# Selective-scan kernel: a Sign whose loops are exchanged, and a copy of partial sums issued one place earlier on ScalarE

## The chip, the cores and the metric

One core of one Trainium2 chip. The metric is device time in microseconds (us); the executions of one kernel on one chip spread over 0.05% to 0.43%, mostly over 0.3% or less. Each kernel was run beside the kernel before on the same chip, in alternating rounds; the kernel before has medians of 5773.73 to 5782.82 us by chip, so comparisons are made within rounds. Engines in profiles: PE is TensorE's matmuls, PEld its weight loads, DVE VectorE, ACT ScalarE, POOL GpSimd, SP SyncE.

## The reference, cut to what matters

The network has a binarised convolution block with a selective scan, then linear attention and a small feed-forward part, on 4 images of 64 x 64 pixels and 96 channels. The change touches two places:

```python
t = prelu(conv3x3(sign(xc)) + b) + xc          # 192 channels, 4096 pixels an image
xconv = silu(t)                                # u of the scan
x_dbl = sign(xconv) @ Wb.T + b                 # only the SIGN of xconv feeds the projections

h = exp(delta * A) * h + (delta * u) * B       # the scan along the 4096 pixels, 4 directions, 192 x 16 states
y = sum over the 16 states of h * C
```

## The kernel before

A work item ("piece") of the scan is one tile of 128 x 1024: 32 channels by 4 states on the partitions, 1024 pixels. There are 1536 pieces. Per piece i:

```python
if i >= 1: self.carry(i - 1)            # ACT copies the last column of h(i-1): waits for scan i-1
if i + 1 < n: self.decay(i + 1)         # ACT: dA = exp(delta * A), into one of two PSUM tiles
full = i % 8 == 3 and i > 8
if full: self.evacuate(i - 4)           # ACT copies 8 pieces' sums of y out of their PSUM bank
elif i >= 3: self.reduce(i - 3)         # PE sums over the states into that bank
if i + AHEAD < n: self.inject(i + AHEAD)  # POOL: w = (delta * u) * B
self.scan(i)                            # DVE: the scan; then w = h * C on DVE or on POOL
...
interleave(lanes); next(back, None)     # background: one step of other stages' work
if full: self.reduce(i - 3)             # in a full iteration the sums come last
```

Who computes `w = h * C` is decided while the program is built: a tally of modelled times gives it to the less loaded of VectorE and GpSimd (905 and 631 of the 1536). The "background" holds the convolutions of the next images and the epilogues of earlier ones, in steps between pieces. The first image's convolution has nothing to hide under: no scan can start before it ends.

The convolution works through 16 parts an image (96 channels x 512 pixels, 18 matmuls each). For each part, while the next part's matmuls are issued:

```python
vector: pz = pz * s + v;  pz = r * (1 - a) + pz
scalar: sg = Sign(pz)     -> fp8 bytes, even and odd pixels of 64 put apart    # the changed line
scalar: e = Exp(-pz); e = Ln(e + 1); e = Exp(-e)                               # sigmoid
vector: u = pz * e
...                       # then, for the part whose matmuls have ended:
vector or scalar: v = ...;  scalar: r = Relu(...)       # read the matmuls' result
```

## Time and profile before

| | before |
|---|---|
| time | 5783.25 us (5775.27 to 5783.98, 3 runs) |
| first convolution, start of first to end of last part | about 83 to 217 us |
| scans | 288 to 5610 us |
| VectorE and GpSimd busy in the scans | 94% each |
| ScalarE busy in the scans | 65% |
| the Sign | 64 x 2.484 us = 159 us of ScalarE |

The table is read by asking, for each stage, who ends it. The prediction does that, with the lines.

### The profile page before, as it was taken

To read this page: it belongs to the slowest core of one execution; us is meant where nothing else is said; L and a number is where in the kernel's file an instruction comes from. 1 tells how busy PE (TensorE), PEld (TensorE's weight loads), DVE (VectorE), ACT (ScalarE), POOL (GpSimd) and SP (SyncE) were. 2 spreads that over 40 slices of the span, in tenths; PEclk is the share of its full clock that TensorE was granted. 3 is DMA by queue.
4 is the path that set the end of the run, shared out by engine and by line. 5 is a ranking of instruction groups with operands and counts; after the bars stand their busy time and mean duration, and the time that the engine had idled before them with its cause. 6 is when DMAs were issued, how large, how long until landed. Compare 5 with 4: busy or idle time off the path is not lost. (4 is left out here: it accounts for less than half of the span.)

```text
span 5775.5 us, 61921 instructions
## 1 busy us (share of the span) xinstructions
PE 3419.4 (59%) x19813; PEld 1339.9 (23%) x19813; DVE 5176.7 (90%) x3422; ACT 3672.1 (64%) x5620; POOL 5080.7 (88%) x2291
## 2 busy tenths in 40 slices
PE   6446645664468755666446875563477654353577
PEld 3222222222223322222212322221122211111123
DVE  3299999999889999999999999999999999999984
ACT  5567876886556566788655656755556676554544
POOL 2099999999889999999998999999999999999980
PEclk8666755676678866666567885565688765565687
DMA  4455656655676655665567665575667555575652
GB/s 75 105 169 189 196 180 200 194 170 178 200 222 213 205 177 176 204 189 164 184 218 226 209 206 177 182 223 190 207 195 214 191 189 185 174 222 180 197 160 73
DMA packets 589452, 1069.91 MB, mean 185 GB/s; under 512 B 225867, under 2 KB 295556, under 8 KB 587332
## 3 DMA queue, kind: packets, MB, share of 16 engines
q1 hardware_dynamic: 575636, 1065.88, 59.3%
q8 instruction: 156, 2.56, 0.2%
q10 hardware_dynamic: 13488, 0.07, 0.1%
q14 instruction: 172, 1.41, 0.1%
HBM read 833.20 MB, written 229.38 MB: 184 GB/s over the span
## 5 line engine op out<-in xcount | busy, mean ns | idle before, releaser
L386 POOL TENSOR_TENSOR w<-dl,bc 128x1024 f32<-128x1024 f32 x1536 | 3578.4, 2354 | 149.2 <-PE yp L1264 73.8
L1223 ACT ACTIVATE dA<-dl,anm 128x1024 f32<-128x1024 f32 x1536 | 1714.0, 1116 | 494.6 <-DVE w L386 254.6
L1264 PE MATMUL yp<-w,sum 128*32 128x256 f32 x12288 | 1323.3, 547 | 845.8 <-ACT ys L1276 447.7
L386 DVE TENSOR_TENSOR_SCAN dA<-dA,cy,w 128x1024 f32<-128x1024 f32 x680 | 1593.1, 2343 | 109.7 <-ACT dA L1223 94.0
L386 POOL TENSOR_TENSOR w<-h,bc 128x1024 f32<-128x1024 f32 x631 | 1483.8, 2352 | 191.6 <-DVE h L386 181.0
L386 DVE TENSOR_TENSOR w<-dA,bc 128x1024 f32<-128x1024 f32 x905 | 1108.6, 1225 | 57.9 <-DVE dA L386 0.9
L386 DVE TENSOR_TENSOR_SCAN h<-dA,cy,w 128x1024 f32<-128x1024 f32 x472 | 1103.8, 2340 | 12.0 <-ACT dA L1223 10.2
L1264 PEld LDWEIGHTS yp<-w,sum 128*32 128x32 f32 x12288 | 363.1, 137 | 1941.0 <-issue 836.8
L386 DVE TENSOR_TENSOR_SCAN dA<-dA,w 128x1024 f32<-128x1024 f32 x225 | 513.6, 2283 | 38.3 <-ACT dA L1223 29.9
L1254 ACT COPY cy<-dA 128x1 f32<-128x1 f32 x680 | 105.8, 156 | 666.2 <-DVE w L386 665.7
L562 PE MATMUL cv<-tp,cw 96*96 96x512 fp8e5 x1152 | 390.8, 499 | 137.5 <-ACT r L611 110.0
L386 DVE TENSOR_TENSOR_SCAN h<-dA,w 128x1024 f32<-128x1024 f32 x159 | 362.3, 2279 | 32.0 <-POOL w L386 23.7
L562 PEld LDWEIGHTS <-cw 96*96 96x96 fp8e5 x1152 | 174.3, 158 | 358.2 <-issue 314.6
L744 PE MATMUL tn<-yt,ident 96*96 96x512 f32 x256 | 175.1, 820 | 111.8 <-DMA yt<-yd 111.1
L836 PE MATMUL ys<-ey,ident 96*96 96x512 f32 x336 | 184.7, 692 | 75.2 <-DMA ey<-yd 47.4
L1254 ACT COPY cy<-h 128x1 f32<-128x1 f32 x472 | 87.6, 186 | 193.5 <-DVE h L386 193.5
L575 ACT ACTIVATE sg<-cz 96x512 fp8e5<-96x512 f32 x64 | 159.0, 2484 | 22.1 <-DVE cz L386 22.0
L1166 ACT ACTIVATE pd<-dps,dbias,pvd 128x512 f32<-128x512 f32 x189 | 143.7, 760 | 23.1 <-PE dps L1161 23.1
L386 DVE TENSOR_TENSOR u<-cz,e 96x512 f32<-96x512 f32 x64 | 43.8, 684 | 115.6 <-ACT e L586 108.6
L1167 ACT ACTIVATE sp<-dps,dbias,pvd 128x512 f32<-128x512 f32 x189 | 144.6, 765 | 0.0
L836 PE MATMUL fc<-x,mean 96*96 96x512 f32 x54 | 51.9, 1064 | 151.9 <-DVE x L386 151.9
L386 DVE TENSOR_TENSOR pd<-dps,pu 128x512 f32<-128x512 f32 x189 | 130.7, 691 | 8.6 <-DMA pu<-ud 2.2
(305 smaller groups left out, 4448.1 us busy)
## 6 DMA issues: line engine op xcount, KB each, us to landing
dl<-dld SPq DMA_DIRECT2D x768, 512.0 KB
bc<-bcd SPq DMA_DIRECT2D x512, 512.0 KB
dld<-pd SPq DMA_DIRECT2D x126, 512.0 KB
yd<-ys SPq DMA_DIRECT2D x768, 64.0 KB
dld<-pd SPq DMA_DIRECT2D x126, 256.0 KB
yt<-yd SPq DMA_DIRECT2D x128, 192.0 KB
ey<-yd SPq DMA_DIRECT2D x58, 384.0 KB
pu<-ud SPq DMA_DIRECT2D x32, 512.0 KB
```

Source lines behind the costliest of these rows:

```text
L386: return getattr(self.eng, name)(out, *args, **kw)
L562: nc.tensor.matmul(ps, c.cw[:, j, t, 96 * h : 96 * h + 96], tpad[j][:, 8 * q + dy : 8 * q + dy + 8, dx : dx + IW], start=(j == 0 and t == ...
L575: nc.scalar.activation(sg.bitcast(F8).rearrange("p (h e i) -> p h i e", h=8, e=2), pz.rearrange("p (h i e) -> p h i e", h=8, e=2), AF.Sign ...
L744: nc.tensor.matmul(ps, c.i96, t, start=(i == 0), stop=(i == 1))
L836: self.c.nc.tensor.matmul(ps, w, x, start=(i == 0), stop=(i == len(pairs) - 1))
L1166: nc.scalar.activation(d[:, 0], ps, AF.Abs, scale=sc, bias=bi)
L1167: nc.scalar.activation(t, ps, AF.Relu, scale=sc, bias=bi)
L1223: c.nc.scalar.activation(t, self.dlt[i // NQ][0], AF.Exp, scale=c.anm[:, g, NQ * KORD[e] + q : NQ * KORD[e] + q + 1])
L1254: self.c.nc.scalar.copy(self.carries[g, q], h[:, CH - 1 : CH])
L1264: c.nc.tensor.matmul(y[32 * x : 32 * x + 32, g % 2, :], c.sum4, prod[:, 256 * x : 256 * x + 256], start=(q == 0), stop=(q == NQ - 1), tile ...
```

## The change

Intent: the Sign wrote its bytes strided (0, 32, 1, 33, ...) while it read PSUM in order; now it writes bytes in order and reads every second word. And the copy of the sums of y goes ahead of the next exponential, so that TensorE gets the bank sooner; the sums then return to their usual place.

```diff
-  sg.bitcast(F8).rearrange("p (h e i) -> p h i e", h=8, e=2),
-  pz.rearrange("p (h i e) -> p h i e", h=8, e=2), AF.Sign, saturate=False,
+  sg.bitcast(F8).rearrange("p (h e i) -> p h e i", h=8, e=2),
+  pz.rearrange("p (h i e) -> p h e i", h=8, e=2), AF.Sign, saturate=False,
...
             if i >= 1:
                 self.carry(i - 1)
+            if i % 8 == 3 and i > 8:
+                self.evacuate(i - 4)
             if i + 1 < n:
                 self.decay(i + 1)
-            full = i % 8 == 3 and i > 8
-            if full:
-                self.evacuate(i - 4)
-            elif i >= 3:
+            if i >= 3:
                 self.reduce(i - 3)
...
             next(back, None)
-            if full:
-                self.reduce(i - 3)
```

## The prediction

> **What bounds the kernel now.** I read, in this order: the page's table of busy shares, the table of windows (to cut the run into stages), the groups of ScalarE by form, the waits of VectorE and GpSimd, and the timeline around single Signs.
>
> The windows (columns after the stretch: PE, PEld, DVE, ACT, POOL busy, then clock and DMA):
>
> ```profile
> 83.00:217.00 134.00, 91.65 (x313) 46.04 (x312) 47.24 (x64) 79.76 (x82) 16.82 (x16) 0.79 0.23 47
> 288.00:5610.00 5322.00, 3156.90 (x18742) 1202.56 (x18741) 5026.65 (x3152) 3456.04 (x5310) 5023.65 (x2178) 0.67 0.61 193
> 1080.00:1330.00 250.00, 156.31 (x876) 60.90 (x875) 226.92 (x160) 204.12 (x264) 225.97 (x98) 0.70 0.58 177
> ```
>
> From 288 to 5610 us the scans run, and VectorE and GpSimd are each busy 94% of it (5026.65 and 5023.65 of 5322). The products are divided between these two while the program is built, so they finish together; a gain in this stage must shorten both. What is left to win there is their idle time, 295 us each, much of it one waiting for the other. ScalarE, which the change touches, is busy 65%: its time counts only where VectorE waits for it. The 134 us of the first convolution are another stage: nothing else runs yet, and its chain counts in full.
>
> ```profile
> L575 ACT ACTIVATE sg<-cz 96x512 fp8e5<-96x512 f32 x64 | 159.0, 2484 | 22.1 <-DVE cz L386 22.0
> L583 ACT ACTIVATE e<-cz 96x512 f32<-96x512 f32 x64 | 59.9, 936 | 0.0
> L598 ACT COPY ut<-u 96x512 f32<-96x512 f32 x48 | 52.9, 1101 | 41.9 <-DVE u L386 41.9
> L671 ACT ACTIVATE sgn<-acc,sbR 128x512 fp8e5<-128x512 f32 x64 | 49.4, 772 | 0.0
> L611 ACT ACTIVATE r<-cv,cbias,csc 96x512 f32<-96x512 f32 x64 | 49.0, 766 | 35.2 <-DVE v L608 29.4 <-issue 5.8
> L585 ACT ACTIVATE e<-e 96x512 f32<-96x512 f32 x64 | 39.7, 621 | 0.5
> L746 ACT COPY yh<-tn 96x512 f32<-96x512 f32 x64 | 36.9, 577 | 54.4 <-PE tn L744 44.6 <-DMA bc<-bcd 6.8 <-issue 3.0
> ```
>
> The Sign to be changed (L575) takes 2484 ns for 512 elements a lane, where every other activation of that size takes 577 to 772. It runs 64 times: 16 in the first convolution, 48 under the scans. Who waits for it, over the whole run:
>
> ```profile
> DVE u L386 <- ACT e L586: 108.6, 43, 4.3
> DVE dA L386 <- ACT dA L1223: 123.9, 82, 8.5
> PE yp L1264 <- ACT ys L1276: 447.7, 106, 10.6
> POOL w L386 <- PE yp L1264: 74.3, 33, 5.9
> ```
>
> Line 1 is the chain behind the Sign (Exp, Ln, Exp, then u on VectorE): 64.3 us of it lie in the first convolution (15 waits, by the same view for 90 to 225 us), 44.3 us under the scans. Lines 2 to 4 concern the second part of the change: ScalarE's copy of the sums of y holds TensorE up for long, but TensorE is busy only 59%, and only what passes on to GpSimd or VectorE costs time.
>
> [...] The Sign writes single bytes 32 bytes apart[...]. The new Sign reads PSUM with a step of 8 bytes[...]: L671 reads PSUM with a step of 128 bytes and writes runs of 16 bytes in 772 ns, against 766 for L611, which reads and writes in order; L746 reads PSUM 256 bytes apart in 577. [...] the Ln of L585 has 621. So I take 0.61 us for the new Sign.
>
> **The change, part by part: the Sign.** Same function, same 64 calls, same bytes; only the loops are exchanged, so that writing goes in order and reading steps over every second word of PSUM. What it saves on ScalarE I read from starts, since records overlap:
>
> ```profile
> 146.47 2.45 ACT L575 ACTIVATE sg<-cz 96x512 fp8e5<-96x512 f32 x1 [0.94 <-DVE cz L386]
> 148.42 0.92 ACT L583 ACTIVATE e<-cz 96x512 f32<-96x512 f32 x1
> 149.38 0.63 ACT L585 ACTIVATE e<-e 96x512 f32<-96x512 f32 x1
> 150.04 0.63 ACT L586 ACTIVATE e<-e 96x512 f32<-96x512 f32 x1
> ```
>
> From the Sign's start to the Ln's start pass 149.38 - 146.47 = 2.91 us. The Exp's 0.92 holds about 0.3 us of waiting for the Sign's last writes (a like one, the last line, has 0.63). After the change the two should take 0.61 + 0.65 = 1.26 us. Saved: 1.65 us a part, 106 us of ScalarE over 64 parts. Busy time falls by more, as overlaps are counted twice: 64 x (2.48 - 0.61) = 120 us of Sign and 64 x 0.3 = 19 us of Exp.
>
> In the first convolution the parts follow each other in one chain (r, cz, Sign, Exp, Ln, Exp, u, v, r) of 7.4 us, unless the 18 matmuls of the part take longer. By the timeline these take 4.1 us in 7 parts, 5.8 in 4 and 6.8 to 7.4 in 5, as the granted clock goes; matmuls plus v and r (1.65 us) make 5.75, 7.45 and about 8.7 us. So the saving counts where they took 4.1 us, and once at the end, after the last part: 8 x 1.65 = 13 us. A busier TensorE may get less clock, so I take 11.
>
> Under the scans a Sign counts through the wait of u:
>
> ```profile
> 1098.72 2.34 DVE L386 TENSOR_TENSOR_SCAN h<-dA,cy,w 128x1024 f32<-128x1024 f32 x1
> 1100.98 2.33 DVE L386 TENSOR_TENSOR_SCAN dA<-dA,cy,w 128x1024 f32<-128x1024 f32 x1
> 1103.35 1.22 DVE L386 TENSOR_TENSOR w<-dA,bc 128x1024 f32<-128x1024 f32 x1
> 1106.81 0.69 DVE L386 TENSOR_TENSOR u<-cz,e 96x512 f32<-96x512 f32 x1 [2.24 <-ACT e L586]
> ```
>
> ScalarE did the Sign from 1099.89, the Exp from 1101.86, and then without a gap the carry (1102.69), an exponential, the copy of the sums, four activations, up to 1106.78. With the fix the Exp ends near 1101.1, where it meets the end of the scan (1101.06) that the carry needs: so 1.57 us are won of the wait of 2.24, and 0.67 stays. Cutting every such wait by at most 1.57: 9.1 of the 9.5 us in 500 to 760, 14.0 of 18.6 in 1080 to 1330, 13.0 of about 18 in 2500 to 2750 (one wait there is put down to a DMA but is of this kind), together 36 us. GpSimd must follow: in 1080 to 1330 it idles 24 us, 22.2 of them waiting for VectorE's h, so it can give back about as much, but not all at the same moments. I take three quarters: 28 us.
>
> **The copy of the sums.** In one iteration of eight (192 in all) the copy (0.58 us) goes ahead of the next exponential instead of behind it, and the matmuls of sums that need its bank return to their usual place, ahead of the background's matmuls. No instruction is added, and the division of products between VectorE and GpSimd is the same in both programs (VectorE has 3418 rows in each, GpSimd 2237). Where the product before is on VectorE (905 of 1536), the exponential waits 1.2 us for it anyway, and the copy fits in: free. Where it is on GpSimd, the exponential starts 0.6 us later but has the 2.34 us of a scan for its 1.12, so it is in time unless ScalarE is behind. TensorE gets its bank 1.1 to 2.3 us sooner, which shortens part of the 74.3 us that GpSimd waits for it. Against that, where ScalarE is behind, VectorE gets its dA up to 0.58 us later, and background matmuls now stand behind matmuls that wait for the copy. About 15 us won, about 10 lost: I take 5.
>
> Sum: 11 + 28 + 5 = 44 us; 5783 - 44 = 5739.
>
> **The rivals.** (a) Reading PSUM with a step of 8 bytes costs as L598's reading of SBUF does: the Sign then takes about 1.1 us, saves 1.15 us a part, and some 30 us are won in all. L671 and L746 speak against it. (b) VectorE's waits go but GpSimd sets the pace: under the scans both have the same 5025 us of work, so u's wait turns into a wait for w or h, and only the first convolution's 11 us and a few more are won: about 5765. For it speaks the equal load; against it, that GpSimd's idle time in these stretches is nearly all waiting for VectorE. (c) The order does more than I think: TensorE's 447.7 us of waiting for the copy hold background matmuls up, whose results ScalarE waits for in order, with the exponentials behind them. If a third of the 142 us in which the scans wait for dA went (94.0, 10.2, 29.9 and 7.7 us in the groups of their four forms), 5700 would be near. Against it: the long ones (8.49, 7.25, 8.40 us) follow DMAs and matmuls of the epilogue. (d) The copy, now ahead of the exponential, waits for TensorE, which waits for GpSimd's products; then dA comes late, and the 5 us turn into a loss of 10 to 30. The copy waited only 8.6 us in 5 cases before, which speaks against more.
>
> **Range and chances.** Rival (b) or (d) gives the upper end, (c) the lower: 5705 to 5768, with 5739 in the middle. Faster by over 2% would need 5667, that is 116 us: all of the first convolution's 13, all 44 of u's waits and some 60 us from the order. I give it 5%. Slower by over 2% would need a new wait of over 110 us: 1%. Within 2%: 94%.
>
> **What would show it.** The Sign's group at about 0.61 us and the Exp's near 0.64; ScalarE's busy time lower by about 139 us; the scans' start 11 us earlier (near 277); u's waits down from 108.6 to about 50, nearly all in the first convolution (2.6 us a part); VectorE's waits for dA near their 142 us; TensorE's wait for the copy well below 447.7. A Sign of 1.0 us or more proves (a); u's waits gone but GpSimd's or VectorE's other waits up by as much, (b); dA's waits down by over 40 us, (c); dA's up, and the copy waiting for TensorE, (d).

## The result, and the profile after

The changed kernel takes 5721.65 us (5713.14 to 5725.88, 4 runs) against 5782.82 us before in the same rounds: ratio 0.9895, 95% interval 0.9878 to 0.9912, about 61 us. A ratio is the mean time of one kernel's runs over that of the other's of the same rounds, so it is not quite the ratio of the medians. On another chip the changed kernel, run again beside the kernel before, gave 0.9919 (0.9904 to 0.9933), about 47 us. The two intervals overlap; a gain of about 51 to 56 us is what both allow. The verdict at 2% is "same"; that the kernel is faster is clear of noise.

The same groups of ScalarE after the change (Sign and the Exp behind it):

```profile
L575 ACT ACTIVATE sg<-cz 96x512 fp8e5<-96x512 f32 x64 | 37.6, 587 | 22.1 <-DVE cz L386 22.0
L583 ACT ACTIVATE e<-cz 96x512 f32<-96x512 f32 x64 | 37.4, 584 | 0.0
```

The Sign went from 2484 to 587 ns, the Exp from 936 to 584: the Exp, which is itself unchanged, had been held up by the Sign before it. Next, when the first scan starts, before and then after (start in us first; the bracket is idle time and what ended it):

```profile
287.85 2.29 DVE L386 TENSOR_TENSOR_SCAN h<-dA,w 128x1024 f32<-128x1024 f32 x1 [16.84 <-POOL w L386]
```

```profile
261.79 2.29 DVE L386 TENSOR_TENSOR_SCAN h<-dA,w 128x1024 f32<-128x1024 f32 x1 [16.87 <-POOL w L386]
```

26.1 us are won before any scan runs, where the prediction had 11. (The other traces with the new Sign and no filling, in the table below, have their first scan between 259.4 and 265.6 us: 22 to 28 us.) The windows of the changed kernel, first convolution and scans:

```profile
83.00:191.00 108.00, 78.49 (x312) 41.27 (x311) 47.98 (x64) 50.46 (x82) 16.83 (x16) 0.90 0.28 59
262.00:5546.00 5284.00, 3175.24 (x18742) 1172.35 (x18741) 5013.06 (x3151) 3370.88 (x5310) 5023.77 (x2177) 0.67 0.61 195
```

The stage of the first convolution took 134 us and takes 108; its granted clock rose from 0.79 to 0.90. The scans took 5322 us and take 5284, with the same work of GpSimd (5023.65 and 5023.77). The waits after the change:

```profile
PE yp L1264 <- ACT ys L1276: 562.7, 133, 9.6
POOL w L386 <- DVE h L386: 186.9, 180, 4.3
DVE dA L386 <- ACT dA L1223: 128.3, 88, 7.0
DVE u L386 <- ACT e L586: 55.9, 35, 2.5
POOL w L386 <- PE yp L1264: 37.3, 26, 5.0
```

VectorE's wait for the chain behind the Sign fell from 108.6 to 55.9 us; 39.8 of the rest lie in the first convolution (16 waits of 2.5). GpSimd's wait for TensorE's sums halved (74.3 to 37.3), but its wait for VectorE's h rose from 181.0 to 186.9, and TensorE's wait for the copy did not fall, as forecast, but rose from 447.7 to 562.7.

The same moment under the scans that the prediction showed with a wait of 2.24 us, one convolution part after the change, VectorE and then ScalarE:

```profile
1062.39 2.33 DVE L386 TENSOR_TENSOR_SCAN dA<-dA,cy,w 128x1024 f32<-128x1024 f32 x1
1064.75 1.22 DVE L386 TENSOR_TENSOR w<-dA,bc 128x1024 f32<-128x1024 f32 x1
1066.62 0.69 DVE L386 TENSOR_TENSOR u<-cz,e 96x512 f32<-96x512 f32 x1 [0.65 <-ACT e L586]
```

```profile
1061.31 0.58 ACT L575 ACTIVATE sg<-cz 96x512 fp8e5<-96x512 f32 x1
1061.78 0.59 ACT L583 ACTIVATE e<-cz 96x512 f32<-96x512 f32 x1
1062.50 0.19 ACT L1254 COPY cy<-h 128x1 f32<-128x1 f32 x1
1062.60 0.58 ACT L1276 COPY ys<-yp 128x512 f32<-128x512 f32 x1
1063.08 1.12 ACT L1223 ACTIVATE dA<-dl,anm 128x1024 f32<-128x1024 f32 x1
```

The wait of u is 0.65 us (forecast 0.67): Sign and Exp now end (1062.37 us) before the scan that the carry waits for (1062.47), and the rest of the chain can't start sooner. Here the copy of the sums stands ahead of the exponential, as the change wants it.

### The profile page after: what moved, and what is told of

It is laid out like the page before. It is cut to its first block, busy times and chain, and to the rows that moved or that the text cites.

```text
span 5711.4 us, 61936 instructions
## 1 busy us (share of the span) xinstructions
PE 3423.4 (60%) x19813; PEld 1304.6 (23%) x19813; DVE 5164.2 (90%) x3422; ACT 3558.0 (62%) x5620; POOL 5081.2 (89%) x2291
## 5 line engine op out<-in xcount | busy, mean ns | idle before, releaser
L1264 PE MATMUL yp<-w,sum 128*32 128x256 f32 x12288 | 1346.8, 544 | 992.3 <-ACT ys L1276 562.7
L386 POOL TENSOR_TENSOR w<-h,bc 128x1024 f32<-128x1024 f32 x631 | 1483.5, 2351 | 201.3 <-DVE h L386 186.9
L1264 PEld LDWEIGHTS yp<-w,sum 128*32 128x32 f32 x12288 | 336.6, 134 | 2134.7 <-issue 751.4
L562 PE MATMUL cv<-tp,cw 96*96 96x512 fp8e5 x1152 | 378.9, 484 | 93.1 <-ACT r L611 83.1
L386 DVE TENSOR_TENSOR dps<-dps,sp 128x512 f32<-128x512 f32 x189 | 129.1, 683 | 0.0
L889 ACT COPY ysum<-ys 96x512 f32<-96x512 f32 x56 | 32.5, 581 | 154.6 <-PE ys L836 154.5
```

What stands on the lines that cost most here:

```text
L386: return getattr(self.eng, name)(out, *args, **kw)
L562: nc.tensor.matmul(ps, c.cw[:, j, t, 96 * h : 96 * h + 96], tpad[j][:, 8 * q + dy : 8 * q + dy + 8, dx : dx + IW], start=(j == 0 and t == ...
L889: nc.scalar.copy(t, ps)
L1264: c.nc.tensor.matmul(y[32 * x : 32 * x + 32, g % 2, :], c.sum4, prod[:, 256 * x : 256 * x + 256], start=(q == 0), stop=(q == NQ - 1), tile ...
```

## The experiments

After the result, my theory was: the first convolution won more than forecast because TensorE slows down when it idles between parts, and a shorter chain lets it idle less; the order is worth little. Rivals: the order carries a good part of the gain; or TensorE's clock is a budget of work, and the faster matmuls came from elsewhere.

| run | Sign | order | what else | median us | before us, same rounds | ratio (95% interval) | first scan starts |
|---|---|---|---|---|---|---|---|
| changed kernel | new | new | | 5721.65 | 5782.82 | 0.9895 (0.9878 to 0.9912) | 261.8 |
| s1_sign_only | new | old | | 5729.54 | 5776.71 | 0.9910 (0.9895 to 0.9926) | 259.9 |
| s2_order_only | old | new | | 5773.99 | 5776.71 | 0.9996 (0.9983 to 1.0008) | 286.9 |
| s3_sign_head | new in the first convolution | old | | 5747.96 | 5776.71 | 0.9952 (0.9940 to 0.9965) | 259.4 |
| s4_before_filled | old | old | 4 filling matmuls a part | 5772.08 | 5776.71 | 0.9997 (0.9980 to 1.0013) | 283.8 |
| f8_before_filled8 | old | old | 8 filling matmuls a part | 5766.71 | 5773.73 | 0.9989 (0.9980 to 0.9998) | 280.3 |
| r1_after | new | new | | 5724.17 | 5773.73 | 0.9919 (0.9904 to 0.9933) | 265.6 |
| r2_sign_only | new | old | | 5722.29 | 5773.73 | 0.9917 (0.9903 to 0.9932) | 260.9 |
| w2_after_filled | new | new | 4 filling matmuls a part | 5719.17 | 5773.73 | 0.9911 (0.9896 to 0.9925) | 255.7 |
| o1_copy_first | new | first half | | 5722.56 | 5775.94 | 0.9903 (0.9887 to 0.9918) | 261.7 |
| o2_sums_early | new | second half | | 5712.01 | 5775.94 | 0.9888 (0.9873 to 0.9904) | 263.2 |
| w3_after_filled | new | new | as w2 | 5717.36 | 5775.94 | 0.9894 (0.9879 to 0.9910) | 254.0 |

All of these gave right results. Kernels of one before-value ran on one chip.

### The two halves of the change apart

The Sign alone: the kernel before with the first hunk of the diff only.

> Only the Sign is changed, the order stays as before. Theory: the Sign carries nearly all of the gain: the scans start 26 us earlier (near 262 us), another 30 us are won where the other three convolutions run under the scans, together 5727 us (-56), and the change of order is worth the rest, 3 to 8 us. Rival: the order carries a third or more of the 61 us (by holding TensorE up less), then this run stays above 5740. VectorE's waits for u should fall from 108.6 to about 56 us as in the changed kernel.

Measured: 5729.54 us, ratio 0.9910; first scan at 259.9 us; VectorE's waits for u 59.5 us. That is 47 us by the medians and 52 by the ratio: the Sign carries nearly all of it.

The order alone: the kernel before with the other hunks only.

> Only the order is changed, the Sign stays as before. Theory: the scans start at 288 us as before, GpSimd's wait for TensorE's sums halves (74 to about 37 us), VectorE's waits for dA stay near 142 us, and the time falls by 3 to 8 us, to about 5777. Rival 1: the order alone is worth 20 us or more (5762 or less). Rival 2: it is worth nothing or costs some us by itself, since dA comes up to 0.58 us later (5783 to 5790).

Measured: ratio 0.9996, an interval from 10 us faster to 5 us slower; first scan at 286.9 us. GpSimd's wait for TensorE's sums did halve, and its wait for VectorE rose by nearly as much:

```profile
PE yp L1264 <- ACT ys L1276: 587.6, 134, 9.6
POOL w L386 <- DVE h L386: 210.8, 185, 4.3
POOL w L386 <- PE yp L1264: 34.0, 25, 5.3
```

Against before (447.7, 181.0, 74.3 in the same lines), GpSimd waits 40 us less for TensorE and 30 us more for VectorE. It reached the next thing it had to wait for. Rival 1 falls; whether the order is worth 3 us or nothing, this run can't tell.

So the two were run again side by side.

> The changed kernel again, on the same chip and in the same rounds as the kernel with the Sign alone, to weigh the change of order. From the earlier chips: ratio to before near 0.9895.

> The Sign alone again. If the order is worth something once the Sign is in order, the changed kernel beside it is faster by 5 to 12 us (in the traces so far its last scan starts 11 us earlier); if the order is worth nothing, the two differ by less than 4 us.

Measured: 0.9919 (the 0.9895 expected from the first chip was missed) and 0.9917. With the Sign in order, the kernel with the change of order comes out 1 us slower, with an uncertainty of some 8 us each way. The 11 us by which the changed kernel's last scan started earlier in the first traces was a difference of executions.

### Where the Sign's gain lies

The new Sign in the first convolution only:

```diff
-  sg....rearrange("p (h e i) -> p h i e", ...), pz.rearrange("p (h i e) -> p h i e", ...)
+  sg....rearrange("p (h e i) -> p h e i" if alone else "p (h e i) -> p h i e", ...),
+  pz.rearrange("p (h i e) -> p h e i" if alone else "p (h i e) -> p h i e", ...)
```

> The Sign is changed in the first convolution alone (16 of 64), order as before. Theory: the scans start 26 us earlier, near 262 us, with the matmuls of most parts at 4.1 us, and all of it reaches the end: 5757 us. Rival: the gain of the start is partly given back under the scans (DMAs and stages meet differently), then 5765 or more. VectorE's waits for u under the scans stay near 44 us.

Measured: 5747.96 us, ratio 0.9952, 28 us by the ratio (20 to 35 by its interval); first scan at 259.4 us, 28 us earlier. So what is won before the scans reaches the end, as far as this interval can tell. The rest of the Sign's gain, s1 against s3 in the same rounds, is 18 us by the medians and 24 by the ratios, with an uncertainty of some 9 us: it belongs to the three convolutions under the scans, where VectorE's waits for u fell from 46.5 us in s3 to 19.8 in s1 (16.1 in the changed kernel). So most of the 27 us of waiting removed there became time: two thirds to nine tenths of it by these two figures.

### Why the first convolution won 26 us and not 11

The prediction took the duration of a part's matmuls as given. Before, TensorE's timeline reads (start, duration of the 18 matmuls, idle before):

```profile
90.76 4.08 PE L562 MATMUL cv<-tp,cw 96*96 96x512 fp8e5 x18 [1.60 <-ACT r L611]
94.68 0.38 PE L613 MATMUL cz<-xsT,winT 96*96 96x512 fp8e5 x1
98.11 6.80 PE L562 MATMUL cv<-tp,cw 96*96 96x512 fp8e5 x18 [3.05 <-ACT r L611]
104.75 0.38 PE L613 MATMUL cz<-xsT,winT 96*96 96x512 fp8e5 x1
```

After:

```profile
90.85 4.08 PE L562 MATMUL cv<-tp,cw 96*96 96x512 fp8e5 x18 [1.60 <-ACT r L611]
94.77 0.38 PE L613 MATMUL cz<-xsT,winT 96*96 96x512 fp8e5 x1
96.64 4.09 PE L562 MATMUL cv<-tp,cw 96*96 96x512 fp8e5 x18 [1.49 <-ACT r L611]
100.56 0.38 PE L613 MATMUL cz<-xsT,winT 96*96 96x512 fp8e5 x1
```

A fast part (4.08 us) ended early, waited 3.05 us for the chain, and the next part ran slow (6.80 us). After the change the wait is 1.49 us, and the next part is fast too (4.09 us): 11 of 16 parts take 4.1 us, the others 5.8 to 6.3, none more. To test idle time apart from the Sign, I gave TensorE matmuls that nobody reads, in the kernel before:

```diff
                         pz, c.winT[:, 96 * h : 96 * h + 96], xsT[:, 512 * q : 512 * q + 512], start=True, stop=True
                     )
+                    if alone:
+                        fill = p.ps.tile([128, 512], F32, ..., tag="y")[0:96]
+                        for _ in range(4):       # 8 in f8_before_filled8
+                            nc.tensor.matmul(fill, c.winT[:, 0:96], xsT[:, 512 * q : 512 * q + 512], start=True, stop=True)
```

> The kernel before, both parts undone, with four more matmuls of 512 columns after each part of the first convolution, into a bank that nobody reads, so that TensorE idles about 1 us less between parts. Theory: TensorE slows down because of its idle time of over 3 us between parts; filled, the 18 matmuls of nearly all parts take 4.1 us instead of up to 7.4, the parts then follow ScalarE's and VectorE's chain of 7.44 us, and the scans start 6 to 7 us earlier (near 281 us). Rival (the one of the prediction): more work on TensorE costs clock; then as many parts as before or more take 5.8 to 7.4 us and the scans start at 288 us or later.

> The kernel before with eight matmuls of filling after each part, so that TensorE's gap between fast parts falls from 3.0 to about 1.2 us. Idle theory: no part at 6.8 us or above any more, at most 5 at 5.8 us, and the scans start 6 to 7 us before 288 us, as four matmuls of filling gave 4 us. Rival (budget): slower parts than with four, and a start at 288 us or later.

Measured with four: 10 parts at 4.1 us (before 7), 3 at 5.8, 3 at 6.4 to 7.4; first scan 4 us earlier, at 283.8. Less than expected, but in the direction of idle time and against the budget. With eight it is plain:

```profile
105.14 4.08 PE L562 MATMUL cv<-tp,cw 96*96 96x512 fp8e5 x18 [1.35 <-ACT r L611]
109.06 0.38 PE L613 MATMUL cz<-xsT,winT 96*96 96x512 fp8e5 x1
109.28 1.89 PE L619 MATMUL fill<-xsT,winT 96*96 96x512 fp8e5 x8
112.53 4.08 PE L562 MATMUL cv<-tp,cw 96*96 96x512 fp8e5 x18 [1.36 <-ACT r L611]
116.45 0.38 PE L613 MATMUL cz<-xsT,winT 96*96 96x512 fp8e5 x1
```

All parts but the first take 4.1 us, at the old chain's period of 7.4 us (112.53 - 105.14); the first scan starts at 280.3, 7.6 us earlier, and the kernel takes 0.9989 of before (6 us, interval just clear of 1). The windows of 83 to 190 us, before and then with eight, show the granted clock behind POOL's count:

```profile
83.00:190.00 107.00, 78.70 (x267) 39.39 (x266) 37.74 (x51) 64.86 (x67) 12.61 (x12) 0.81 0.25 50
```

```profile
83.00:190.00 107.00, 88.97 (x393) 48.75 (x392) 40.16 (x55) 67.71 (x70) 13.66 (x13) 0.98 0.27 55
```

0.81 against 0.98, by more work and less idle time. The budget rival falls.

The record of the granted clock in the kept traces says more. In this stage the clock is either 1.0 or 0.5 and changes on a grid of 3.413 us: its stretches last 3.41, 6.83 or 10.24 us in the kernel before (86 to 210 us), and 3.41, 10.24 or 27.31 us in the changed kernel (87 to 186 us). Counted over the windows of this grid from 84 to 205 us in all 14 traces: at full clock, a window in which TensorE was busy under 53% was followed by one at half clock in all of 29 cases; from 53 to 55% in 40 of 44; from 55% up in none of 282. At half clock, full clock came back after 58 of the 59 windows that were busy throughout, and after 1 of the 66 others. (Under the scans the same count is less sharp: in the kernel before, half clock followed 232 of 239 windows busy under 53% and 2 of 272 from 55% up; full clock came back after 191 of 250 windows busy for 99% or more and after 49 of the 791 others.) So by this count what slows a part is no single gap, but a window with too much idle time in it. All six gaps of over 3 us in the kernel before did it; one of 1.55 us that falls whole into one window, which is then idle for 45%, did it in 4 of 5 cases in the changed kernel: there the window from 111.19 to 114.60 us has TensorE busy for 1.86 of its 3.41 us, and the next has half clock. With eight matmuls of filling no window ahead of the last part's end was busy under 58%. This count was made after the runs, and no run was made to test it.

The same filling in the changed kernel, which beats it if the slow parts that are left go too:

> The changed kernel with four matmuls of filling after each part of the first convolution. Idle theory: the parts whose 18 matmuls still take 5.8 us (5 of 16) come to 4.1 us, the scans start up to 8 us earlier (near 254 us), and the time falls by as much. Rival (TensorE's clock is a budget of work): more parts at 5.8 us or above and a later start of the scans.

> The changed kernel with four matmuls of filling again, to see whether its lead holds: the scans start near 256 us, ratio to before 0.991 or below if the 6 to 10 us that the start wins reach the end; near 0.992 if they are given back under the scans.

Measured: in w2's trace all parts but the first at 4.1 us and a period of 5.8; the first scan at 255.7 and 254.0 us, 6 to 12 us earlier than the changed kernel's 261.8 and 265.6. In time: 0.9911 beside the changed kernel's 0.9919 in the same rounds, and 0.9894 on another chip. That is the right sign, but intervals overlap: the earlier start is in both traces, a shorter time isn't shown.

This also puts the 26 us together. With TensorE always fast, a part takes 7.4 us with the old Sign (f8) and 5.8 with the new (w2): 1.6 us x 16 parts = 26 us. The slow matmuls cost about 7.6 us before (f8 against before) and 6 to 10 us after (w2 against the changed kernel), so they about cancel.

### The halves of the change of order

The Sign in order, and first only the copy moved ahead of the exponential:

```diff
+            full = i % 8 == 3 and i > 8
+            if full:
+                self.evacuate(i - 4)
             if i + 1 < n:
                 self.decay(i + 1)
-            full = i % 8 == 3 and i > 8
-            if full:
-                self.evacuate(i - 4)
-            elif i >= 3:
+            if i >= 3 and not full:
                 self.reduce(i - 3)
```

then only the sums moved ahead of the background (the copy stays behind the exponential):

```diff
             if full:
                 self.evacuate(i - 4)
-            elif i >= 3:
+            if i >= 3:
                 self.reduce(i - 3)
...
-            if full:
-                self.reduce(i - 3)
```

> Sign in order, and of the change of order only its first half: the copy goes ahead of the exponential, the sums stay behind the background's matmuls. Theory of a cancellation: the copy ahead delays dA, so VectorE's waits for dA rise by about 10 us as in the changed kernel, while GpSimd's waits for TensorE fall; then the two halves have opposite signs and one of these two runs is slower than the Sign alone (ratio 0.9917) by 5 us or more and the other faster. Rival: neither half moves the time by more than 5 us, as what one engine no longer waits for it waits for elsewhere: both ratios within 0.9909 to 0.9925.

> Sign in order, and of the change of order only its second half: the sums go ahead of the background's matmuls, the copy stays behind the exponential. Theory of a cancellation: TensorE is held up longest here (its waits for the copy above the 563 us of the changed kernel), but dA isn't delayed; see the run before. Rival: within 0.9909 to 0.9925 too.

Measured: 0.9903 and 0.9888. Both lie below the window that I had named from another chip, and so does w3, which on that other chip had 0.9911 and here 0.9894; so the chip, or its kernel before, accounts for some of it. Their own intervals overlap: in time the two runs are inconclusive, and a lead of the second half over both together, if there is one, is not shown. Neither half came out slower than the Sign alone, as the theory of a cancellation wanted, but the Sign alone was not run in these rounds. The waits are clear, and they put GpSimd's gain into the other half than the expectation of o1 had it. The copy first:

```profile
PE yp L1264 <- ACT ys L1276: 309.8, 72, 9.2
POOL w L386 <- DVE h L386: 153.7, 156, 5.9
POOL w L386 <- PE yp L1264: 72.3, 36, 6.1
```

The sums early:

```profile
PE yp L1264 <- ACT ys L1276: 754.9, 154, 10.7
POOL w L386 <- DVE h L386: 180.0, 187, 3.6
POOL w L386 <- PE yp L1264: 38.4, 20, 4.9
```

It is the place of the sums that halves GpSimd's wait (38.4), although TensorE waits longest there (754.9); the copy ahead shortens TensorE's wait (309.8) and leaves GpSimd's alone (72.3). And the copy ahead costs VectorE something: counting its waits for dA in the traces by the place of the piece in its group of eight, the piece after the copy has

```
                 before  s1    o2    |  changed  r1    o1    s2    w3
wait for dA, us   29.1   28.4  29.4  |  39.7     42.6  36.9  34.7  36.8
```

The traces left out of this table fit: 23.0 to 31.4 us without the copy ahead (s3, s4, f8, r2), 38.3 with it (w2). Between kernels of the same rounds (s2 against s1, r1 against r2, o1 against o2) it is 6 to 11 us more with the copy ahead.

### How the Sign's cost depends on its access pattern

In the changed kernel the eight groups of rows got eight forms of the Sign, eight calls each; its results are wrong.

> Wrong results on purpose: in the changed kernel the Sign of the eight groups of rows uses eight forms, eight calls each. Reading PSUM in order, with a step of 8 bytes, or of 128 bytes, always writing bytes in order: theory 587 ns each (a step in PSUM costs ScalarE nothing); rival: the step costs, then the first is faster than 587 ns and the third slower. Writing single bytes with a step of 2, 8, 16, 32 bytes, reading in order: [...] rival: any write that is not in order costs the same, 2.4 us from a step of 2 on. The old form again: 2.45 us.

Measured (it ran once; the line numbers are its own; groups of ScalarE by form):

```profile
L577 ACT ACTIVATE sg<-cz 96x512 fp8e5<-96x512 f32 x8 | 4.7, 588 | 2.9 <-DVE cz L386 2.9
L579 ACT ACTIVATE sg<-cz 96x512 fp8e5<-96x512 f32 x8 | 4.7, 585 | 2.1 <-DVE cz L386 2.1
L581 ACT ACTIVATE sg<-cz 96x512 fp8e5<-96x512 f32 x8 | 4.7, 588 | 3.1 <-DVE cz L386 3.1
L583 ACT ACTIVATE sg<-cz 96x512 fp8e5<-96x512 f32 x8 | 4.7, 590 | 2.6 <-DVE cz L386 2.6
L585 ACT ACTIVATE sg<-cz 96x512 fp8e5<-96x512 f32 x8 | 10.6, 1321 | 3.1 <-DVE cz L386 3.1
L587 ACT ACTIVATE sg<-cz 96x512 fp8e5<-96x512 f32 x8 | 19.6, 2455 | 2.5 <-DVE cz L386 2.5
L589 ACT ACTIVATE sg<-cz 96x512 fp8e5<-96x512 f32 x8 | 19.0, 2374 | 3.4 <-DVE cz L386 3.3
L591 ACT ACTIVATE sg<-cz 96x512 fp8e5<-96x512 f32 x8 | 19.8, 2472 | 2.5 <-DVE cz L386 2.5
```

The first three write in order and read PSUM in order, with a step of 8 bytes, and of 128 bytes: 588, 585, 588 ns. So a step of 8 or 128 bytes in PSUM costs ScalarE nothing here. The next four read in order and write bytes with a step of 2, 8, 16, 32: 590, 1321, 2455, 2374 ns; the last line is the old form, 2472. From a step of 16 on the cost is flat (2455 and 2374 ns); a step of 2 costs no more than order (590 against 588), but a step of 8 isn't free: it costs 2.2 times as much. So the rival, 2.4 us from a step of 2 on, falls. In time a byte (the mean over 512) that is 1.15 ns with a step of 2, 2.6 with 8 and 4.8 with 16. What sets the cost between these steps isn't shown; a step of 4 was not run.

## Why the prediction was right or wrong

**The Sign's duration: right.** 587 ns for 610 forecast, which was my estimate beside the Ln's 621; rival (a), a costly step in PSUM, is ruled out by the probe (585 and 588 ns with a step, 588 in order). The prediction's "every other activation of that size takes 577 to 772" overlooks two lines of its own view, L598 (1101, a copy that reads SBUF 256 bytes apart) and L583 (936); nothing rests on it. From the Sign's start to the Ln's 1.11 us pass in the first convolution (0.49 and 0.62 between starts), so 1.80 us a part are won on ScalarE for 1.65 forecast.

**ScalarE's busy time: wrong by a double count.** It fell by 114 us, not 139. I had subtracted two groups whose records overlap; the page's total counts overlapping time once. 64 x 1.80 = 115 us is the measure.

**The first convolution: the chain right, the clock wrong.** The step that failed is "the saving counts where they took 4.1 us" with "a busier TensorE may get less clock, so I take 11". Measured 26.1 us. The prediction took the duration of each part's matmuls as fixed, and had the clock fall with work. In these traces it fell with idle time: a window of 3.41 us in which TensorE was busy under 53% was followed by one at half clock in all of 29 cases, and shorter gaps raised the clock (0.79 to 0.90). Each of the 16 parts was won in effect, not 8. One limit did move: at 5.8 us a part, TensorE's 4.1 us plus v and r (1.65 us) set the period, and no longer ScalarE's chain.

**u's waits under the scans: right, somewhat too large.** 36 us of waiting were to go, and 30 did; the wait shown fell to 0.65 (forecast 0.67). (One sum is off: eight waits cut by at most 1.57 give 12.6 us in 2500 to 2750, not 13.0; 36 stands.) Three quarters were to become time, 28 us; measured 18 to 24 of 27 us, s1 against s3. Rival (b), GpSimd setting the pace, is refuted in its strong form; that it takes the remaining share is a guess.

**The order: wrong.** Forecast 5 us from 15 won and 10 lost; measured nothing, within about 8 us. The step that failed is that an earlier bank "shortens part of the 74.3 us that GpSimd waits for it" and that TensorE's wait for the copy would be "well below 447.7". It rose to 562.7, as the sums now reach the wait before the background's matmuls do, and GpSimd's gain came from the place of the sums and was mostly waited away for VectorE. The loss, a later dA after the copy, is there (6 to 11 us of VectorE's waiting). Rival (c) falls, since VectorE's waits for dA didn't shrink (142 us before, 152 after); of (d), the late dA is real, but the copy waited little for TensorE (8.6 us before, 18.1 after).

Sum: forecast 11 + 28 + 5 = 44 us; by the parts 26 + 18 to 24 + 0 = 44 to 50; measured 47 and 61 us on two chips. That the total came near is in part luck: one term was too small (11 for 26) and two too large (28 for 18 to 24, 5 for nothing). Why the first chip shows some 10 us more than the parts is not settled; the spread of executions (5765 to 5779 us for the kernel before within one set of rounds) is as large.

## What to carry to other kernels

When ScalarE writes single bytes to SBUF, let the write run in order and put the stride on the PSUM side: that took this instruction from 2484 to 587 ns. Take a matmul's duration in a chain with gaps as a result of the gaps and not as a constant (the same 18 took 4.1 to 7.4 us here), and check it by filling the gaps with matmuls that nobody reads (with eight, all parts but the first took 4.1 us). Here it was enough that TensorE was busy for 55% or more of each window of 3.41 us: none of 282 such windows at full clock was followed by half clock. Before counting a removed wait as time, ask what its engine meets next: GpSimd waited 40 us less for TensorE and 30 us more for VectorE.
